# Source rows of a graph layer: the 45 tiles read row by row through SyncE go to GpSimd's gathers

## The chip, the core and the metric

The kernel runs on one core of a Trainium2 chip. The metric is the device time of one launch in microseconds. The chip's engines are named as the profile names them: PE (TensorE, matmuls; PEld is its weight load), DVE (VectorE), ACT (ScalarE), POOL (GpSimd) and SP (SyncE, which only issues DMAs here).

## The reference, cut to what matters

```
h   = relu(layernorm(x))                       # x: 12500 nodes x 48
tmp = concat([h[dst], h[src], edge_attr], 1)   # 400000 edges, dst sorted
msg = relu(tmp @ W1 + b1) @ W2 + b2            # W1: 128 x 128, W2: 128 x 48
out = x + segment_sum(msg, dst, 12500)
```

The edges are sorted by `dst`; `src` is random. So whatever depends on `dst` can be read in windows of neighbouring nodes, and whatever depends on `src` has to be picked node by node.

## The kernel before

**Two tables.** A first stage (`node_tables`, lines 92 to 232) normalizes the nodes and multiplies them by the two halves of W1. It leaves `tab_a` (destination half) and `tab_b` (source half), each one row of 128 numbers per node, in DRAM, and the source half a second time, turned, as `bt` in SBUF: 128 partitions, one column per node.

**Chunks.** The second stage (`windows`, lines 235 to 527) takes the edges in 3125 tiles of 128, eight tiles to a chunk, 391 chunks. For chunk c, SP loads a window of 80 rows of `tab_a` (`rhs`, line 362), the edge attributes (`lhs`, line 367) and the destinations (`row`, line 369). DVE makes one-hot windows of the destinations (`lhs`, line 383, and `hot`, line 388). PE multiplies `lhs` and `rhs` (line 401), which gives the destination and edge parts of eight tiles in PSUM (`pre`). The source part is added (lines 420 to 424), ACT applies relu (line 425), PE folds the edges into the 80 nodes of the window (`p_g`, lines 433 and 438), and DVE adds the window to a running segment (line 452). Segments of twelve chunks are multiplied by W2 and stored (lines 456 to 484).

**Three ways to the source rows of a tile.** The change is about these.

- *Gathers.* POOL issues one indirect DMA for a tile: 128 rows of `tab_b`, picked by the indices `srci`, go to one tile's place in `gb` (lines 375 to 381). 2719 tiles take this way. The pool of `gb` has six buffers of a chunk each, so POOL can start a chunk's gathers when `hid`, six chunks earlier, has read its buffer.
- *Columns.* In most chunks the last tile is put together from `bt`: each copy moves one column, at an address taken from a register, into `gt` (line 353). DVE does 59 of a chunk's 119 copies and ACT 60, and PE turns the tile onto `pre` (line 411). 361 tiles take this way (`BYCOLS`); their source part is in `pre` already, and ACT applies the relu straight from there (line 424).
- *Single rows.* SP reads one row of 512 bytes of `tab_b` into one partition of `gs`, with the address from a register (lines 314 to 325). It does 15 such DMAs in each chunk (`RPART`), so a tile of 128 rows is complete every eight or nine chunks. 45 tiles take this way (`BYROWS`, 5760 DMAs), and DVE adds such a tile by an instruction of its own (line 422).

**Numbers.** The registers are loaded from a table `last` in SBUF, one row of `WIDTH` int32 per chunk (line 304, at most 32 numbers a load). In a row stand the 119 column places, the base of the window and the 15 rows' nodes for SP (from `BASE` = 120 on), and four numbers for the segments. `SEG0` is the SBUF byte address of the first segment, which the tables' sizes shift.

**Order.** The order in each engine is written out by hand (lines 486 to 527): the loop body of chunk c issues `prepare(c)` (SP loads, gathers, one-hots, DVE's first 23 column copies), then the single rows of c, DVE's other column copies, the matmuls of c-1 and the fold of c-2, ACT's first 28 copies, `hidden(c-1)` (lines 415 to 426), ACT's other 32 copies and `add(c-2)`. The gathers that POOL issues meanwhile are for a chunk five or six further on.

Of the kernel before, what the change touches and what calls it, by code (L numbers as in the profile page):

```python
# [8 lines left out]
F32 = mybir.dt.float32  # L9
# [7 lines left out]
P = 128  # L17
N, D, DE, HID, E = 12500, 48, 32, 128, 400000
# [4 lines left out]
T = 8  # L23
# [20 lines left out]
U8 = mybir.dt.uint8  # L44
# [3 lines left out]


COLS = 1  # L50
ROWS0 = 1
END = NT // T


# [3 lines left out]
)  # L58
PART = sum(n for _, _, n, _ in PARTS)
BASE = 120  # L60
RPART = 15

BT0 = 16512
SEG0 = 122144
SEG_SIZE = 8 * L


SEG, NEXT, SEG2 = 136, 137, 138
PLACE0 = 139
WIDTH = 140  # L70
SLOTS = (NCH + 2 + P - 1) // P
MOST = 32

# [1 line left out]
def tiles_of(first, part):  # L75

    n = (END - first) * part // P
    return [first + (P * (j + 1) + part - 1) // part - 1 for j in range(n)]


BYCOLS = tiles_of(COLS, PART)
BYROWS = tiles_of(ROWS0, RPART)
EPS = 1e-5


# [149 lines left out]
def windows(nc, tc, gp, bt, ident, idx, x_t, tab_a, tab_b, dst, edge_t, w1, w2s, b2s, out_t):  # L235
# [3 lines left out]
    with ExitStack() as es:  # L239
# [5 lines left out]
        gtp = es.enter_context(tc.tile_pool(name="gtp", bufs=3))  # L245
# [13 lines left out]
        for _, _, n, at in PARTS:  # L259
# [1 line left out]
                last[:, :, at : at + n], last[:, :, at : at + n], 4, BT0,  # L261
                op0=ALU.mult, op1=ALU.add,
            )
        rows_at = slice(BASE, BASE + 1 + RPART)
        nc.vector.tensor_scalar(
            last[:, :, rows_at], last[:, :, rows_at], 4 * HID, None, op0=ALU.mult
        )
        tab8, taba8 = (t.rearrange("n h -> (n h)").bitcast(U8) for t in (tab_b, tab_a))

        place = PARTS[0][3] - 1  # L270
        for a, b in ((place, SEG2), (NEXT, SEG)):
# [5 lines left out]
        nc.vector.scalar_tensor_tensor(  # L277
            last[:, :, at_place], last[:, :, at_place], 4.0, last[:, :, PLACE0 : PLACE0 + 1],
            op0=ALU.mult, op1=ALU.add,
# [8 lines left out]
            rhss.append(rhs)  # L288
        st = {}
        gts = {}  # L290
        gss = {}

        def group(c):

            return divmod(c + OFF, GQ)
# [4 lines left out]
        def numbers(c, at, n, engine):  # L300

            got = []
            for k in range(0, n, MOST):
                got += nc.values_load_multi_w_load_instructions(  # L304
                    last[c % P : c % P + 1, c // P, at + k : at + min(k + MOST, n)],
                    engines=[engine], min_val=0, max_val=1 << 23,
                    skip_runtime_bounds_check_because="numbers of nodes, and what is made of them",
                )[1]
            return got

        def node(n):
            return n.with_bounds(min_val=0, max_val=N - 1)

        def rows(c, nodes):

            for k, n in enumerate(nodes):
                e = (c - ROWS0) * RPART + k
                of = BYROWS[e // P]
                if of not in gss:
                    gss[of] = gtp.tile([P, HID], F32, name="gs")  # L320
                n = n.with_bounds(min_val=0, max_val=4 * HID * (N - 1))
                nc.sync.dma_start(  # L322
                    gss[of].bitcast(U8)[e % P : e % P + 1, :],
                    tab8[bass.ds(n, 4 * HID)].rearrange("(o h) -> o h", o=1),
                )

        regs = {}

# [12 lines left out]
        def columns(c, part):  # L341

            dve, first, _, _ = PARTS[part]
            copy = nc.vector.tensor_copy if dve else nc.scalar.copy
            for k, at in enumerate(regs.pop((c, part), [])):
                j, e = divmod((c - COLS) * PART + first + k, P)
                of = BYCOLS[j]
                if of not in gts:
                    gts[of] = gtp.tile([HID, P], F32, name="gt")
                at = at.with_bounds(  # L350
                    min_val=BT0, max_val=BT0 + 4 * (N - 1), guaranteed_mod_val=0, out_of_modulus=4
                ) - BT0
                copy(gts[of][:, e : e + 1], bt8[:, bass.ds(at, 4)].bitcast(F32))  # L353

        def prepare(c):
            n = min(T, NT - c * T)
            at = c * CE
            m = max(0, min(RPART, len(BYROWS) * P - (c - ROWS0) * RPART)) if c >= ROWS0 else 0
            base, *nodes = numbers(c, BASE, 1 + m, mybir.EngineType.SP)
            rhs = rhss[c % 3]  # L360
            base = base.with_bounds(min_val=0, max_val=4 * HID * (N - 1))
            nc.sync.dma_start(
                rhs.bitcast(U8)[:W, :],
                taba8[bass.ds(base, 4 * HID * W)].rearrange("(w h) -> w h", w=W),
            )
            lhs = ld.tile([P, CE], F32, name="lhs")
            nc.sync.dma_start(lhs[W:K, : n * P], edge_t[:, at : at + n * P])
            row = ld.tile([W, CE], I16, name="row")
            nc.sync.dma_start(
                row[:, : n * P],  # L370
                dst[at : at + n * P].rearrange("(o e) -> o e", o=1).to_broadcast([W, n * P]),
            )
            st[c] = dict(n=n, rows=nodes)
            gb = gp.tile([P, T, HID], F32, name="gb")
            for t in range(n - (c in BYCOLS) - (c in BYROWS)):
                nc.gpsimd.indirect_dma_start(  # L376
                    out=gb[:, t, :], out_offset=None, in_=tab_b[:, :],
                    in_offset=bass.IndirectOffsetOnAxis(
                        ap=srci[:, c * T + t : c * T + t + 1], axis=0
                    ),  # L380
                )

            nc.vector.tensor_scalar(  # L383
                lhs[:W, : n * P], row[:, : n * P], bw[:, c : c + 1], None, op0=ALU.is_equal,
            )
            columns(c, 0)
            hot = wp.tile([P, T, W], F32, name="hot")
            nc.vector.tensor_tensor(  # L388
                hot[:, :n, :], wnum.unsqueeze(1).to_broadcast([P, n, W]),
                rel[:, c * T : c * T + n].unsqueeze(2).to_broadcast([P, n, W]), op=ALU.is_equal,  # L390
            )
            load(c, 1)
            st[c].update(rhs=rhs, lhs=lhs, gb=gb, hot=hot)
# [21 lines left out]
        def hidden(c):  # L415
            s = st[c]
            n, m, pre = s["n"], s["added"], s["pre"]
            h = wp.tile([P, T, HID], F32, name="hid")
            g = m - (c in BYROWS)
            nc.vector.tensor_add(h[:, :g, :], pre[:, :g, :], s["gb"][:, :g, :])  # L420
            if g < m:
                nc.vector.tensor_add(h[:, g, :], pre[:, g, :], gss.pop(c))
            if m < n:
                nc.scalar.activation(h[:, m, :], pre[:, m, :], AF.Relu)  # L424
            nc.scalar.activation(h[:, :m, :], h[:, :m, :], AF.Relu)  # L425
            s["h"] = h
# [16 lines left out]
        def add(c):  # L443

            s = st.pop(c)
            k = group(c)[0] % 2
            of = SEG0 + k * SEG_SIZE
            at = s["base"].with_bounds(
# [33 lines left out]
        def segment_store(g, n):  # L482
            first, = numbers(begin(g), SEG, 1, mybir.EngineType.SP)
            nc.sync.dma_start(out_t[:, bass.ds(node(first), n)], xs.pop(g)[:, :n])

        with tc.manual_schedule():
            for c in range(NCH + 2):
                if c < NCH:
                    prepare(c)
                    rows(c, st[c].pop("rows"))  # L490
                if c >= NCH:
                    columns(c, 0)
                columns(c, 1)
                load(c, 2)
                columns(c, 2)
                if 0 <= c - 1 < NCH:
                    before(c - 1)
                if 0 <= c - 2 < NCH:
                    fold(c - 2)
                if 0 <= c - 1 < NCH:  # L500
                    turned(c - 1)

                g, k = group(c - 2)
                if k == GQ - 3 or c == NCH - 1:
                    segment_load(g)
                if g > 0 and k < L // BLK:
                    segment_sum(g - 1, k, BLK)
                if g > 0 and k == STORE:
                    segment_store(g - 1, L)
                columns(c, 3)  # L510
                if 0 <= c - 1 < NCH:
                    hidden(c - 1)
                load(c + 1, 0)
                load(c, 4)
                columns(c, 4)
                if 0 <= c - 2 < NCH:
                    add(c - 2)
                    if k == GQ - 1:
                        segment_next(g)
                load(c + 1, 3)  # L520
                if c == NCH + 1:
                    segment_sum(g, 0, END_L)
                    segment_store(g, END_L)

                if c < PIECES:
                    s = slice(c * PIECE, (c + 1) * PIECE)
                    nc.sync.dma_start(out_t[:, s], x_t[:, s])
# [126 lines left out]
def tile_gnn_preln(  # L654
# [52 lines left out]
    flag = const.tile([1, 1], I32, name="flag")  # L707
    last = const.tile([P, SLOTS, WIDTH], I32, name="last")

# [157 lines left out]
```

## Time and profile before

| | |
|---|---|
| median of 3 runs | 5037.61 us (5035.85 to 5037.8) |
| the profiled execution | 5046.97 us, span 5045.2 us, granted PE clock 0.643 |
| first `hid` add (line 420) of 391 | at 158.51 us |
| last one | at 5032.55 us |
| busy | PE 63%, ACT 58%, DVE 58%, POOL 53% |
| gathers (line 376) | 2719, 972 ns each |
| SP's single rows (line 322) | 5760 of 0.5 KB |

All but 171 us of the span lies between these two adds: the loop over chunks. This text calls the time from the start of one `hid` add of DVE to the start of the next a **cycle**: one chunk. The 390 cycles have a mean of 12.50 us. No engine is busy for more than two thirds of the span, so the page's sums don't say what bounds the loop, and a cycle has to be read in the timeline. Column copies have a line of their own (353) on ACT and on DVE. "issue" in a wait is idle time in which the engine waited for nothing that the profile shows.

### The profile page before, as it was taken

Reading aid. Unit: us, or ns where it says so; the run is one execution under the profiler, and the core shown is the slowest. Engines: PE = TensorE matmul, PEld = TensorE weight load, DVE = VectorE, ACT = ScalarE, POOL = GpSimd, SP = SyncE. Lnnn points to the kernel's source line nnn. Section 1 sums busy time; section 2 is a strip of 40 time slices with the busy share of each in tenths; the row PEclk is TensorE's granted clock in tenths of the full one; section 3 lists DMA queues with packets and bytes.
Section 4 is the critical chain, followed back from the end, with each engine's and each line's share of the span. In section 5 each row is a group of like instructions: output and inputs, shape, how many; then the busy total and the mean of one; then the engine's idle time right before and its main releaser. Section 6 shows DMA issues by size and latency. Waiting matters only on the chain. (4 is left out here: it accounts for less than half of the span.)

```text
span 5045.2 us, 105760 instructions
## 1 busy us (share of the span) xinstructions
PE 3196.2 (63%) x16917; PEld 2891.6 (57%) x16917; DVE 2915.2 (58%) x24786; ACT 2927.7 (58%) x24107; POOL 2664.5 (53%) x2746
## 2 busy tenths in 40 slices
PE   6565666665666665566666665666666666666676
PEld 4555555555555555556565555556555565555565
DVE  4555555555555555565555555555555565555555
ACT  3455655655555555566565555556565566555555
POOL 5455555555555555555555555555555555555553
PEclk8666666666666666666666666666666666665656
DMA  3422222222222222222222222222222222222221
GB/s 135 123 67 69 68 66 68 68 67 68 64 65 66 68 70 67 64 68 71 67 69 69 68 67 67 69 67 69 67 67 68 69 71 68 68 66 69 66 69 51
DMA packets 202255, 354.44 MB, mean 70 GB/s; under 512 B 70322, under 2 KB 108228, under 8 KB 200276
## 3 DMA queue, kind: packets, MB, share of 16 engines
q0 software_dynamic: 87040, 178.39, 14.2%
q1 hardware_dynamic: 114256, 169.09, 11.3%
q14 instruction: 560, 4.59, 0.3%
q8 instruction: 139, 2.28, 0.2%
q10 hardware_dynamic: 260, 0.10, 0.0%
HBM read 327.84 MB, written 22.07 MB: 69 GB/s over the span
## 5 line engine op out<-in xcount | busy, mean ns | idle before, releaser
L376 POOL DMA_INDIRECT gb<-tab_b,srci x2719 | 2643.0, 972 | 2315.4 <-DVE hid L420 1319.5
L353 ACT COPY gt<-bt 128x1 f32 x23280 | 2477.9, 189 | 1893.8 <-issue 1867.1
L353 DVE COPY gt<-bt 128x1 f32 x22928 | 1704.1, 143 | 1795.4 <-issue 1750.0
L433 PE MATMUL p_g<-hot,hid 128*128 128x80 f32 x6250 | 1392.9, 414 | 1664.1 <-ACT hid L425 1585.3
L433 PEld LDWEIGHTS p_g<-hot,hid 128*128 128x128 f32 x6250 | 1313.3, 320 | 1745.7 <-ACT hid L425 1689.4
L401 PEld LDWEIGHTS pre<-rhs,lhs 112*128 112x128 f32 x6250 | 1149.6, 283 | 92.8 <-issue 85.4
L401 PE MATMUL pre<-rhs,lhs 112*128 112x128 f32 x6250 | 1171.3, 366 | 17.1 <-DVE lhs L383 17.1
L420 DVE TENSOR_TENSOR hid<-pre,gb 128x896 f32<-128x896 f32 (+2 forms) x391 | 420.8, 1076 | 6.8 <-issue 4.4
L425 ACT ACTIVATE hid<-hid 128x896 f32<-128x896 f32 (+1 forms) x391 | 370.8, 948 | 39.3 <-DVE hid L420 38.0
L411 PE MATMUL pre<-ident,gt 128*128 128x128 f32 x722 | 278.7, 489 | 112.0 <-remote 104.9
L388 DVE TENSOR_TENSOR hot<-wnum,rel 128x640 f32<-128x640 f32 x391 | 315.9, 808 | 5.1 <-issue 4.9
L383 DVE TENSOR_SCALAR lhs<-row,bw 80x1024 f32<-80x1024 int16 x391 | 306.8, 785 | 12.8 <-DMA row<-in_dst 7.9
L438 PEld LDWEIGHTS <-ones 128*128 128x128 bf16 x3125 | 291.9, 154 | 0.0
L438 PE MATMUL p_g<-hot,ones 128*128 128x80 bf16 x3125 | 283.7, 265 | 0.0
L411 PEld LDWEIGHTS pre<-ident,gt 128*128 128x128 f32 x722 | 193.4, 328 | 118.4 <-remote 110.6
L452 DVE TENSOR_TENSOR seg<-seg,p_g 128x160 f32 x391 | 125.7, 321 | 191.8 <-DVE hid L420 156.8
L424 ACT ACTIVATE hid<-pre 128x128 f32<-128x128 f32 x361 | 97.5, 270 | 86.8 <-DVE hid L420 78.4
L478 PE MATMUL p_f<-seg,w2s 128*48 128x512 f32 (+1 forms) x134 | 121.0, 1005 | 0.4 <-DVE seg L452 0.4
L479 PE MATMUL p_f<-seg,b2s 1*48 1x512 f32 (+1 forms) x134 | 95.5, 801 | 0.0
L479 PEld LDWEIGHTS p_f<-seg,b2s 1*48 1x48 f32 x134 | 13.1, 143 | 100.8 <-issue 100.8
L468 DVE MEMSET seg<- 128x944 f32 x64 | 54.1, 845 | 9.5 <-issue 0.3
L480 DVE TENSOR_TENSOR xseg<-xseg,p_f 48x512 f32<-48x512 f32 (+1 forms) x67 | 44.8, 668 | 23.3 <-PE p_f L479 22.4
(67 smaller groups left out, 306.3 us busy)
## 6 DMA issues: line engine op xcount, KB each, us to landing
gs<-tab_b SPq DMA_DIRECT2D x5760, 0.5 KB
row<-in_dst SPq DMA_DIRECT2D x390, 160.0 KB
lhs<-in_edge_t SPq DMA_DIRECT2D x390, 128.0 KB
gb<-tab_b,srci POOLq DMA_INDIRECT x2719
rhs<-tab_a SPq DMA_DIRECT2D x391, 40.0 KB
xseg<-in_x_t SPq DMA_DIRECT2D x33, 192.0 KB
out_x<-xseg SPq DMA_DIRECT2D x33, 192.0 KB
tab_b<-tab SPq DMA_DIRECT2D x3, 1280.0 KB
```

The source lines that it names most:

```text
L353: copy(gts[of][:, e : e + 1], bt8[:, bass.ds(at, 4)].bitcast(F32))
L376: nc.gpsimd.indirect_dma_start(out=gb[:, t, :], out_offset=None, in_=tab_b[:, :], in_offset=bass.IndirectOffsetOnAxis(ap=srci[:, c * T + t ...
L383: nc.vector.tensor_scalar(lhs[:W, : n * P], row[:, : n * P], bw[:, c : c + 1], None, op0=ALU.is_equal,)
L388: nc.vector.tensor_tensor(hot[:, :n, :], wnum.unsqueeze(1).to_broadcast([P, n, W]), rel[:, c * T : c * T + n].unsqueeze(2).to_broadcast([P ...
L401: nc.tensor.matmul(pre[:, t, :], s["lhs"][:K, t * P : (t + 1) * P], s["rhs"][:K, :], start=True, stop=c not in BYCOLS or t < n - 1,)
L411: nc.tensor.matmul(s["pre"][:, s["n"] - 1, :], gts.pop(c), ident, start=False, stop=True)
L420: nc.vector.tensor_add(h[:, :g, :], pre[:, :g, :], s["gb"][:, :g, :])
L425: nc.scalar.activation(h[:, :m, :], h[:, :m, :], AF.Relu)
L433: nc.tensor.matmul(p_g[:, 0, :], s["h"][:, t, :], s["hot"][:, t, :], start=t == 0, stop=t == n - 1)
L438: nc.tensor.matmul(p_g[:, 1, :], ones, high[:, t, 1::2], start=t == 0, stop=t == n - 1)
L452: nc.vector.tensor_add(to, to, s["p_g"])
L478: nc.tensor.matmul(p_f[:, :n], w2s, seg[:, 0, s], start=True, stop=False)
```

## The change

The single rows go: `rows()`, its list of tiles `BYROWS`, the 15 extra numbers per chunk that SP loads, and the separate add. The 45 tiles are gathered by POOL as the others are, so there are 2764 gathers. The add of line 422 becomes part of that of line 420. The row of numbers in `last` shrinks from 140 int32 to 128 (of which the base takes one and three are left empty), its segment numbers move, and `SEG0` becomes 192 bytes less (four rows of twelve int32 less on each partition).

```diff
-RPART = 15
-SEG0 = 122144
+SEG0 = 121952
-SEG, NEXT, SEG2 = 136, 137, 138
-PLACE0 = 139
-WIDTH = 140
+SEG, NEXT, SEG2 = 124, 125, 126
+PLACE0 = 127
+WIDTH = 128
...
-        def rows(c, nodes):
-
-            for k, n in enumerate(nodes):
-                e = (c - ROWS0) * RPART + k
-                of = BYROWS[e // P]
-                if of not in gss:
-                    gss[of] = gtp.tile([P, HID], F32, name="gs")
-                n = n.with_bounds(min_val=0, max_val=4 * HID * (N - 1))
-                nc.sync.dma_start(
-                    gss[of].bitcast(U8)[e % P : e % P + 1, :],
-                    tab8[bass.ds(n, 4 * HID)].rearrange("(o h) -> o h", o=1),
-                )
...
-            m = max(0, min(RPART, len(BYROWS) * P - (c - ROWS0) * RPART)) if c >= ROWS0 else 0
-            base, *nodes = numbers(c, BASE, 1 + m, mybir.EngineType.SP)
+            base, = numbers(c, BASE, 1, mybir.EngineType.SP)
...
-            for t in range(n - (c in BYCOLS) - (c in BYROWS)):
+            for t in range(n - (c in BYCOLS)):
                 nc.gpsimd.indirect_dma_start(
...
-            g = m - (c in BYROWS)
-            nc.vector.tensor_add(h[:, :g, :], pre[:, :g, :], s["gb"][:, :g, :])
-            if g < m:
-                nc.vector.tensor_add(h[:, g, :], pre[:, g, :], gss.pop(c))
+            nc.vector.tensor_add(h[:, :m, :], pre[:, :m, :], s["gb"][:, :m, :])
...
-                    rows(c, st[c].pop("rows"))
```

What SP issues early in the loop shows the first place; `rhs`, `lhs` and `row` are the loads of a chunk, `gs` the single rows, and line 304 is the load of the registers. Before, for chunk 1:

```order
L304 TENSOR_LOAD last
L362 DMA rhs_703<-tab_a 80x512
L367 DMA lhs<-in_edge_t 32x1024
L369 DMA row<-in_dst 80x1024
L322 DMA gs<-tab_b 1x512 x15
L527 DMA out_x<-in_x_t 48x1696
```

Of the change, at the same place:

```order
L300 TENSOR_LOAD last
L344 DMA rhs_703<-tab_a 80x512
L349 DMA lhs<-in_edge_t 32x1024
L351 DMA row<-in_dst 80x1024
L505 DMA out_x<-in_x_t 48x1696
```

Nothing else moved in SP's list: 5760 issues have gone from between the loads of one chunk and of the next, and the register load ahead of them reads one number in place of 16.

DVE's part of the loop at the first tile of single rows (chunk 9), before:

```order
L388 TENSOR_TENSOR hot<-wnum,rel 128x640
L304 TENSOR_LOAD last
L353 COPY gt<-bt 128x1 x20
L304 TENSOR_LOAD last
L353 COPY gt<-bt 128x1 x16
L420 TENSOR_TENSOR hid<-pre,gb 128x768
L422 TENSOR_TENSOR hid<-pre,gs 128x128
L304 TENSOR_LOAD last
L452 TENSOR_TENSOR seg_660<-seg_660,p_g 128x2x80
```

Of the change:

```order
L370 TENSOR_TENSOR hot<-wnum,rel 128x640
L300 TENSOR_LOAD last
L336 COPY gt<-bt 128x1 x20
L300 TENSOR_LOAD last
L336 COPY gt<-bt 128x1 x16
L401 TENSOR_TENSOR hid<-pre,gb 128x896
L300 TENSOR_LOAD last
L431 TENSOR_TENSOR seg_660<-seg_660,p_g 128x2x80
```

One add of seven tiles stands where an add of six and one of a single tile stood; the column copies and the register loads of DVE and ACT are the same. In POOL's list the count of gathers in a row goes from 2719 to 2764.

More of the change, by code (lines that the diff above doesn't have):

```diff
@@ L50 @@
 COLS = 1
-ROWS0 = 1
 END = NT // T
@@ L81 @@
 BYCOLS = tiles_of(COLS, PART)
-BYROWS = tiles_of(ROWS0, RPART)
 EPS = 1e-5
@@ L263, in windows @@
             )
-        rows_at = slice(BASE, BASE + 1 + RPART)
+        rows_at = slice(BASE, BASE + 1)
         nc.vector.tensor_scalar(
@@ L267, in windows @@
         )
-        tab8, taba8 = (t.rearrange("n h -> (n h)").bitcast(U8) for t in (tab_b, tab_a))
+        taba8 = tab_a.rearrange("n h -> (n h)").bitcast(U8)
         place = PARTS[0][3] - 1
@@ L290, in windows @@
         gts = {}
-        gss = {}
         def group(c):
@@ L372, in prepare @@
             )
-            st[c] = dict(n=n, rows=nodes)
+            st[c] = dict(n=n)
             gb = gp.tile([P, T, HID], F32, name="gb")
-            for t in range(n - (c in BYCOLS) - (c in BYROWS)):
+            for t in range(n - (c in BYCOLS)):
                 nc.gpsimd.indirect_dma_start(
@@ L827 @@
         numbers[COLS : COLS + len(cols), at : at + n] = cols[:, k : k + n]
-    in_rows = np.array(BYROWS) * T + T - 1 - np.isin(BYROWS, BYCOLS)
-    rows = by_tile[in_rows].reshape(-1)
-    rows = np.pad(rows, (0, -len(rows) % RPART)).reshape(-1, RPART)
-    numbers[ROWS0 : ROWS0 + len(rows), BASE + 1 : BASE + 1 + RPART] = rows
     last = np.ascontiguousarray(numbers.reshape(SLOTS, P, WIDTH).transpose(1, 0, 2))
```

## The prediction

> **What bounds the kernel now.** I read the costliest groups of the page first, then the waits, then single cycles in the timeline.
>
> ```profile
> L376 POOL DMA_INDIRECT gb<-tab_b,srci x2719 | 2643.0, 972 | 2315.4 <-DVE hid L420 1319.5
> L353 ACT COPY gt<-bt 128x1 f32 x23280 | 2477.9, 189 | 1893.8 <-issue 1867.1
> L353 DVE COPY gt<-bt 128x1 f32 x22928 | 1704.1, 143 | 1795.4 <-issue 1750.0
> gs<-tab_b SPq DMA_DIRECT2D x5760, 0.5 KB
> ```
>
> The reader is to see two things. POOL is not saturated: it sits idle for 1319.5 us until a `hid` add gives a buffer back. And the column copies have as much idle time before them as work in them, although they wait for nothing that the profile shows. Where this idle time lies is seen in one cycle. Here is DVE from 1736.74 us, and what SP issues in it:
>
> ```profile
> 1736.74 1.07 DVE L420 TENSOR_TENSOR hid<-pre,gb 128x896 f32<-128x896 f32 x1
> 1740.22 0.81 DVE L388 TENSOR_TENSOR hot<-wnum,rel 128x640 f32<-128x640 f32 x1
> 1741.16 0.58 DVE L353 COPY gt<-bt 128x1 f32 x8
> 1742.37 0.22 DVE L353 COPY gt<-bt 128x1 f32 x2 [0.63 <-issue]
> ...
> 1744.53 0.15 DVE L353 COPY gt<-bt 128x1 f32 x1 [0.52 <-issue]
> ...
> 1747.39 0.15 DVE L353 COPY gt<-bt 128x1 f32 x1 [0.52 <-issue]
> 1748.13 1.18 DVE L353 COPY gt<-bt 128x1 f32 x18 [0.58 <-issue]
> 1749.82 1.08 DVE L420 TENSOR_TENSOR hid<-pre,gb 128x896 f32<-128x896 f32 x1
> ```
> ```profile
> 1738.17 10.48 SPq L322 DMA_DIRECT2D gs<-tab_b  x15
> ```
>
> Eight copies run at full pace (0.58 us for eight). Then, until 1748.13, one or two pass every 0.71 us or so: I call this the **crawl**. It ends at once, and the 18 copies that are left run at full pace up to the `hid` add. ACT's copies show the same steps. SP's 15 single rows take 10.48 us in this cycle, 0.7 us each; six of them outside a crawl took 1.83 us (a row below), 0.3 us each. So SP crawls too.
>
> The crawl goes with the gathers. POOL's gathers follow each other every 1.25 us, and a burst starts when `hid` is done:
>
> ```profile
> 1280.64 0.95 POOL L376 DMA_INDIRECT gb<-tab_b,srci  x1 [5.75 <-DVE hid L420]
> 1281.89 0.94 POOL L376 DMA_INDIRECT gb<-tab_b,srci  x1 [0.30 <-issue]
> ...
> 1288.15 0.95 POOL L376 DMA_INDIRECT gb<-tab_b,srci  x1 [0.30 <-issue]
> 1292.89 0.95 POOL L376 DMA_INDIRECT gb<-tab_b,srci  x1 [3.79 <-DVE hid L420]
> ```
>
> In the next cycle that I show, the crawl ends at 1290.63, 1.53 us after the last of these gathers (1288.15 + 0.95). And in whole cycles (first and last of each kind; the number after x under POOL counts its gathers):
>
> ```profile
> core 0: us, PE busy (x) PEld busy (x) DVE busy (x) ACT busy (x) POOL busy (x), PEclk, DMA share, GB/s
> 170.97:183.87 12.90, 7.74 (x42) 7.55 (x42) 7.37 (x65) 7.54 (x66) 6.89 (x7) 0.62 0.38 103
> 4969.55:4981.66 12.11, 5.52 (x35) 5.08 (x34) 6.84 (x65) 7.52 (x65) 6.89 (x7) 0.64 0.30 83
> 196.25:207.25 11.00, 7.25 (x42) 7.06 (x42) 6.94 (x65) 6.96 (x61) 5.95 (x6) 0.69 0.37 97
> 4908.49:4918.99 10.50, 9.41 (x49) 8.92 (x48) 6.93 (x64) 6.23 (x50) 6.20 (x6) 0.52 0.33 89
> 5000.29:5007.87 7.58, 5.87 (x54) 5.48 (x53) 6.47 (x65) 6.50 (x61) 0.00 (x0) 0.99 0.14 40
> ```
>
> Of all cycles, 323 have seven gathers and a mean of 12.63 us, 39 have six and 11.38 us. Without gathers, at the end of the loop, the same DVE and ACT work takes 7.58 us. So the loop is a ring: `hid` frees a buffer, the burst runs, DVE and ACT crawl through most of it, then finish their copies, and the next `hid` follows. What bounds a cycle is the burst, plus what copies are left when the crawl ends.
>
> **The change part by part.**
>
> *45 more gathers.* Each makes the cycle in which it is issued 1.25 us longer: that is the spacing of two gathers (1281.89 − 1280.64), and also 12.63 − 11.38. 45 × 1.25 = **+56 us**. Nothing hides it, since the burst is on the ring. By the lowest price it is nothing (POOL idles for longer than that), by the highest 1.5 us (12.11 − 10.50 is 1.6): 0 to +72. I take 56, the price of both rows.
>
> The Trainium skill, "Perfetto Trace Analysis", section "Identifying the Most-Contended Engine", judges POOL by its occupancy and would have me optimize the engine with the highest one. By it POOL, the least busy here with 53%, takes the gathers for nothing and the sum below would be 56 us lower; the cycles of six and of seven gathers speak against it.
>
> *45 adds less.* One add of 128x896 takes 1.08 us. The pair that stood in its place is this, at 4981.66 us:
>
> ```profile
> 4981.66 0.95 DVE L420 TENSOR_TENSOR hid<-pre,gb 128x768 f32<-128x768 f32 x1
> 4982.52 0.28 DVE L422 TENSOR_TENSOR hid<-pre,gs 128x128 f32<-128x128 f32 x1
> ```
>
> It ends 1.14 us after its start, so 0.06 us is saved 45 times: **−3 us**. This is on the ring.
>
> *5760 issues less on SP.* Nobody waits for SP by name, as these waits show:
>
> ```profile
> POOL gb L376 <- DVE hid L422: 165.9, 44, 5.7
> DVE lhs L383 <- DMA row<-in_dst: 7.9, 1, 7.9
> DVE lhs L383 <- DMA gs<-tab_b: 4.3, 2, 3.9
> ```
>
> (The first is the ring itself in the chunks of single rows; it will stand under L420's successor.) Taken from waits, SP's work is worth 12 us at most. But SP crawls along with DVE and ACT, and I found cycles in which SP issued nothing. Here SP waits from 1278.1 to 1291.64 us for a segment to store, at the same place of the twelve chunks as the cycle shown above:
>
> ```profile
> 1276.29 1.83 SPq L322 DMA_DIRECT2D gs<-tab_b  x6
> 1291.64 0.35 SPq L484 DMA_DIRECT2D out_x<-xseg  x1
> ```
> ```profile
> 1279.30 1.08 DVE L420 TENSOR_TENSOR hid<-pre,gb 128x896 f32<-128x896 f32 x1
> 1282.69 0.81 DVE L388 TENSOR_TENSOR hot<-wnum,rel 128x640 f32<-128x640 f32 x1
> 1283.61 1.46 DVE L353 COPY gt<-bt 128x1 f32 x20
> ...
> 1290.63 0.40 DVE L353 COPY gt<-bt 128x1 f32 x5 [0.56 <-issue]
> 1291.54 1.07 DVE L420 TENSOR_TENSOR hid<-pre,gb 128x896 f32<-128x896 f32 x1
> ```
>
> With SP quiet, 20 copies pass before the crawl in place of 8, and 5 are left behind it in place of 18. The cycle takes 12.24 us against 13.08. There are five such quiet cycles with seven gathers (first 1279.30, last 4747.59 us): mean 12.32. The other 23 at this place have a median of 12.98: **−0.66 us** for a wholly quiet SP.
>
> After the change SP is not wholly quiet; it still loads a chunk's `rhs`, `lhs` and `row`. What that looks like stands at the end of the trace, when the single rows have run out:
>
> ```profile
> 4951.62 6.34 SPq L322 DMA_DIRECT2D gs<-tab_b  x10
> ...
> 4969.84 0.33 SPq L362 DMA_DIRECT2D rhs<-tab_a  x1
> ...
> 4971.81 0.33 SPq L461 DMA_DIRECT2D xseg<-in_x_t  x1
> ```
>
> The cycle from 4969.55 us (above) has seven gathers and an SP that issues its loads at the start and nothing in the crawl: 12.11 us, where the 267 cycles of seven gathers at the ten ordinary places of twelve have a mean of 12.39: **−0.28 us**. The cycle before it (4957.07 to 4969.55 us), in which SP issued the loads of two chunks, took 12.48 us and shows no gain. So the gain of a cycle lies between 0 and 0.66. I take the nearest rows: 0.28 for the ten ordinary places, whose cycles will look like this one, and 0.66 for the two places (of twelve) where the segment's matmuls lengthen the cycle, which is where the quiet cycles stand. Gathers are issued in 385 cycles: 321 × 0.28 + 64 × 0.66 = 90 + 42 = **−132 us**. At the ends, 0 and 385 × 0.66 = −254.
>
> *The table and the address of the segments.* The register loads of DVE and ACT keep their counts. Shorter rows could change what one load takes:
>
> ```profile
> L304 ACTq TENSOR_LOAD <-last x776: 1695/1932/2829, 134.8 to 5009.0; - x194
> ```
>
> Chunks lie in four rows of 560 bytes on a partition, at four different distances from a round address; the medians of ACT's loads in the first three are 1929, 1923 and 1912 ns. So I count nothing for the 512-byte rows. SP's load of 16 numbers becomes a load of one; SP has the time. The 3 MB that SP read come by POOL's gathers instead, with the same bytes, and the DMA engines are under 40% busy in every cycle shown above.
>
> *Sum.* +56 − 3 − 132 = **−79 us**. The profiled execution took 5046.97 us, 9.4 over the median of the runs. Against the median: 5037.61 − 79 = **4959 us**.
>
> **The rivals.**
>
> *SP's issues cost the others nothing* (the time gets longer). Then the quiet cycles are short for another reason: at that place SP waits just when DVE is late with the segment, so they may have been picked by DVE's own state. For it: the cycle from 4957 us, with SP out of the crawl and no gain. Against it: the 12 more copies before the crawl, in a cycle whose one-hot (`hot`) stands 3.4 us after `hid` as in the other (3.5 us). Price: +56 − 3 = +53, 5091 us. It decides as soon as a quiet SP is worth less than 53/385 = 0.14 us a cycle. The Trainium skill, "DMA: Bandwidth & Descriptors", section "Issuing engines are not separate DMA queues", holds that issuing from several engines only saves time on the sequencer that issues. By that rule SP's time, which nobody waits for, is worth nothing, and 5091 us follows; the quiet cycles of this trace disagree by 0.66 us each.
>
> *The quiet cycle is the rule everywhere.* SP's loads fall outside the crawl, and every cycle gains 0.66: −254 + 53 = −201, 4837 us. For it: some 45 ordinary cycles are over 13.2 us, and in the ones I looked at SP's single rows start early in the burst; these would go. Against it: the cycle from 4969.55.
>
> *All copies fit under the burst.* Then a cycle is 1.34 us to the first gather (1280.64 − 1279.30), 8.46 us to the end of the seventh, 1.53 us to the crawl's end: 11.3 us, and 385 cycles give over 400 us. Against it: ACT has 60 copies of some 0.09 us and two relus of 1.2 us, and does not get through them faster than 12.1 us in the cycle from 4969.55.
>
> *The change does nothing but what hides*, and gain and price cancel: within 0.2%.
>
> **How the numbers follow.** My forecast (4959 us, its own range 4900 to 5020) has 0.55, SP without worth 0.24, the quiet cycle everywhere 0.12, all copies under the burst 0.04, a cancellation 0.05. The range takes in the first three: 4830 to 5095 us. A measurement of this kernel can tell about 0.2% from no change, 10 us. Faster by over that: 0.55 + 0.12 + 0.04, less some of the forecast's upper edge, 0.70; within it 0.06; slower 0.24.
>
> **What would show it.** In the new profile, gathers still 1.25 us apart, 2764 of them, and nearly all cycles with seven. If a quiet SP is worth something, more copies pass on DVE between `hot` and the crawl (over 12), fewer than 10 are left when it ends, and an ordinary cycle is near 12.1 us. If SP is worth nothing, ordinary cycles stay at 12.4 us and the time goes up by the gathers alone. The prediction is wrong in its ground if the crawl no longer ends 1.5 us after the last gather, or if the burst no longer starts with `hid`: then POOL or another engine bounds the loop. If DVE waits for `row`, SP's loads come late.

## The result and the profile after

The changed kernel takes 4972.71 us (median of four runs, 4970.34 to 4976.2) against 5037.7 us before: a ratio of 0.9857, with a 95% interval of 0.9833 to 0.9881, or 65 us less. The profiled execution took 4973.7 us with a span of 4972.0 us. That is 73.2 us less than the span of before, of which 9.3 us are what the profiled execution of before lay above its median.

One fact has to be known before any further number is read. All twelve runs that follow were made on five chips, and on all five the kernel *before* takes 3568 to 3579 us and not 5037 us. There the crawl doesn't appear, and there the change makes the kernel slower. What sets the two conditions apart isn't known, nor whether the chip of before and after is one of the five; I call them the **crawling** condition (the runs of before and of the change above) and the **flowing** one. The granted PE clock is lower in the crawling traces (0.643 and 0.644, against 0.762 and 0.752 in the flowing traces of the same two kernels). By itself that is no mark of the crawl: a slower kernel on a flowing chip, the one with rows of 125 numbers below, gets 0.58 in its slow part, where PE is 48% busy, and 0.76 ahead of it, where PE is 75% busy.

First the crawling condition. The page of the changed kernel, its groups of gathers and copies:

```profile
L358 POOL DMA_INDIRECT gb<-tab_b,srci x2764 | 2682.8, 971 | 2202.5 <-DVE hid L401 1438.1
L336 ACT COPY gt<-bt 128x1 f32 x23280 | 2476.5, 187 | 1843.6 <-issue 1817.5
L336 DVE COPY gt<-bt 128x1 f32 x22928 | 1708.5, 143 | 1715.5 <-issue 1634.7
```

There are 45 gathers more, each as long as before, and POOL still waits for `hid`. Before, that wait was 1319.5 us for the add of line 420 and 165.9 us for that of line 422, 1485.4 us together; now it is 1438.1 us, 47 us less. The copies wait for nothing visible for 115 us less on DVE (1634.7 for 1750.0) and 50 us less on ACT. The timeline shows how. This is DVE in the cycle of the chunk whose cycle the prediction shows for before (the one from 1736.74 us there):

```profile
1703.71 1.08 DVE L401 TENSOR_TENSOR hid<-pre,gb 128x896 f32<-128x896 f32 x1
1705.79 1.47 DVE L336 COPY gt<-bt 128x1 f32 x23
1707.18 0.81 DVE L370 TENSOR_TENSOR hot<-wnum,rel 128x640 f32<-128x640 f32 x1
1708.13 1.34 DVE L336 COPY gt<-bt 128x1 f32 x20
1709.97 0.15 DVE L336 COPY gt<-bt 128x1 f32 x1 [0.51 <-issue]
1710.71 0.21 DVE L336 COPY gt<-bt 128x1 f32 x2 [0.58 <-issue]
...
1714.30 0.15 DVE L336 COPY gt<-bt 128x1 f32 x1 [0.50 <-issue]
1715.00 0.46 DVE L336 COPY gt<-bt 128x1 f32 x6 [0.55 <-issue]
1715.97 1.08 DVE L401 TENSOR_TENSOR hid<-pre,gb 128x896 f32<-128x896 f32 x1
```

POOL's gathers in it, the first and the last of seven:

```profile
1705.05 0.95 POOL L358 DMA_INDIRECT gb<-tab_b,srci  x1 [5.59 <-DVE hid L401]
...
1712.56 0.94 POOL L358 DMA_INDIRECT gb<-tab_b,srci  x1 [0.30 <-issue]
```

After `hot`, 20 copies now pass before the crawl where 8 did, and 6 are left behind it where 18 were. This cycle is one of those with a segment's matmuls; the part on the prediction says how far the others are like it. SP issues nothing between 1703.71 and 1715.97 us, where it issued its 15 rows. The crawl still ends 1.50 us after the last gather (1712.56 + 0.94 to 1715.00). The cycle takes 12.26 us for 13.08.

### The profile page after: what moved, and what is told of

It reads as the page before. It is cut to its first block, busy times and chain, and to the rows that moved or that the text cites. A ratio compares the mean times of both kernels' runs of the same rounds, so it can differ in the third digit from the quotient of the medians.

```text
span 4972.0 us, 94216 instructions
## 1 busy us (share of the span) xinstructions
PE 3217.5 (65%) x16917; PEld 2903.8 (58%) x16917; DVE 2921.8 (59%) x24741; ACT 2925.2 (59%) x24107; POOL 2704.3 (54%) x2791
## 3 DMA queue, kind: packets, MB, share of 16 engines
q1 hardware_dynamic: 102736, 166.09, 11.2%
## 4 chain that ended last, share of the span: by engine, by line
issue 37%; DVE 24%; POOL 21%; ACT 8%; PE 3%; DVEq 3%; DMA 2%; another core or an unknown queue 1%; ACTq 1%; SPq 0%; POOLq 0%
POOL gb L358 21%; DVE gt L336 14%; ACT gt L336 7%; DVE hid L401 3%; DVE lhs L365 3%; DVEq L300 3%; DVE hot L370 2%; DMA gb<-tab_b,srci 1%; ACT hid L404 1%; PE p_g L412 1%; PE p_n L178 1%; PE pre L383 1%; ACTq L300 1%; DVE seg L431 1%
## 5 line engine op out<-in xcount | busy, mean ns | idle before, releaser
L358 POOL DMA_INDIRECT gb<-tab_b,srci x2764 | 2682.8, 971 | 2202.5 <-DVE hid L401 1438.1
L336 DVE COPY gt<-bt 128x1 f32 x22928 | 1708.5, 143 | 1715.5 <-issue 1634.7
L401 DVE TENSOR_TENSOR hid<-pre,gb 128x896 f32<-128x896 f32 (+1 forms) x391 | 426.7, 1091 | 7.8 <-issue 6.7
L393 PE MATMUL pre<-ident,gt 128*128 128x128 f32 x722 | 278.0, 488 | 64.3 <-remote 57.5
```

The lines of the kernel that those rows point to most:

```text
L358: nc.gpsimd.indirect_dma_start(out=gb[:, t, :], out_offset=None, in_=tab_b[:, :], in_offset=bass.IndirectOffsetOnAxis(ap=srci[:, c * T + t ...
L393: nc.tensor.matmul(s["pre"][:, s["n"] - 1, :], gts.pop(c), ident, start=False, stop=True)
L401: nc.vector.tensor_add(h[:, :m, :], pre[:, :m, :], s["gb"][:, :m, :])
```

## The experiments

### Single rows and gathers, each by itself

Four kernels were made from the kernel before. The first drops the rows and keeps the six gathers of the 45 chunks:

```
-                    rows(c, st[c].pop("rows"))
-                nc.vector.tensor_add(h[:, g, :], pre[:, g, :], gss.pop(c))
+                nc.vector.tensor_add(h[:, g, :], pre[:, g, :], zrow)
```

> The kernel before without SP's 5760 single rows; the 45 chunks still gather six tiles and still add in two pieces, the second from a tile of zeros (the source part of these 45 tiles is left out). Theory (SP's issues lengthen the crawl): the change moved the time by -65 us; with +53 us for gathers and adds, the quiet SP is worth -118 us, so 4920 us here, in a span of 4905 to 4935; ordinary cycles of seven gathers near 12.08 us, those of six below the 11.38 us of before. Rival (SP's issues cost the others nothing): 5037 us, and the gain of the change came from gathers taking the place of rows.

The second keeps the rows, into tiles that nobody reads, and gathers and adds as the changed kernel does; the third and the fourth change its rows:

```
-            for t in range(n - (c in BYCOLS) - (c in BYROWS)):
+            for t in range(n - (c in BYCOLS)):
...
-            for k, n in enumerate(nodes):
+            for k, n in enumerate(nodes[:8]):
...
-                    tab8[bass.ds(n, 4 * HID)].rearrange("(o h) -> o h", o=1),
+                    tab8[bass.ds(n, 4 * HID * RPART)].rearrange("(o h) -> o h", o=RPART),
```

> The changed kernel's gathers and adds, with the 15 single rows a chunk still issued by SP into tiles that nobody reads. Theory: the gathers alone, 5037.6 + 53 = 5090 us, or 4973 + 118; ordinary cycles of seven gathers back at 12.39 us. Rival (the issues cost nothing): 4973 us, as changed. Rival (gathers cost nothing, POOL has idle time): 5037 us.

> As the run with all 15 rows added, but with the first eight of a chunk only. Theory, if every issue has the same price: 4973 + 118 x 8/15 = 5036 us. Rival (only issues that reach the crawl cost, and the first six or so pass ahead of it at 0.3 us each): two or three of fifteen count, about 4990 us.

> As the run with all 15 rows added, but the 15 rows are one transfer of 15 neighbouring rows with one issue (the same 7.5 KB in the same 15 lines of 512 bytes). Theory (the instruction on SP is what costs): 4973 + 118/15 = 4981 us. Rival (the transfers cost, by their bytes and packets): 5090 us.

Measured, with the kernel before at 3578.58 us beside them:

| kernel | gathers | SP's rows in a chunk | us | ratio to before (95%) |
|---|---|---|---|---|
| no rows | 2719 | none | 3579.85 | 1.0008 (0.9998 to 1.0017) |
| rows added | 2764 | 15 | 3630.87 | 1.0162 (1.0136 to 1.0189) |
| half of the rows | 2764 | 8 | 3635.95 | 1.0165 (1.0148 to 1.0182) |
| rows as one transfer | 2764 | 1 issue, 15 lines | 3634.43 | 1.0168 (1.0149 to 1.0187) |

In the flowing condition the gathers alone set the time: 52 us more with them (3630.87 − 3578.58), and the three kernels with the same gathers and different rows lie within each other's intervals. The theory's numbers (4920 and 5090 us) can't be compared with these, since the condition is another; of its two terms the gathers' is there and SP's is zero. The rival's ratios (1 for no rows) came true.

### The changed kernel in the flowing condition

> The changed kernel as it is. The four runs so far ran where the kernel before takes 3579 us and shows no crawl: ACT's and DVE's copies keep their pace through the bursts, and SP's rows are issued 0.32 us apart. If the run is made in that condition: theory (the gathers are the bound and cost 1.25 us each, a quiet SP is worth nothing there): 3579 + 53 = 3632 us, slower. If the run is made where the kernel before takes 5037 us: 4973 us, as measured. Rival (the change gains by something that is not the crawl): about 65 us faster in both.

> The kernel before as it is, for a trace in whatever condition this chip has. Where it takes 3570 to 3580 us: no crawl, POOL's gathers nearly back to back, 2719 of them, cycles near 8.83 us against 8.97 of the changed kernel (57 us in 385 cycles). Where it takes 5037 us: the trace of before again.

Measured: 3630.37 us for the change against 3569.88 us, a ratio of 1.0177 (1.0150 to 1.0203): **the change is slower there**, by 60 us. The kernel before took 3568.26 us in its own run. These are two traces to set beside those of the crawling condition. First the groups of the kernel before, flowing:

```profile
L376 POOL DMA_INDIRECT gb<-tab_b,srci x2719 | 2651.9, 975 | 862.7 <-issue 803.4
L353 ACT COPY gt<-bt 128x1 f32 x23280 | 2235.0, 187 | 574.7 <-issue 442.0
L353 DVE COPY gt<-bt 128x1 f32 x22928 | 1497.0, 142 | 263.8 <-issue 223.2
```

A gather and a copy take as long as in the crawling trace (972, 189 and 143 ns there). The unexplained idle time of the copies is 442.0 and 223.2 us in place of 1867.1 and 1750.0, and the largest wait of POOL, for `hid`, is gone: what is left is 0.30 us between two gathers. The chain that ended last says the same, before and changed:

```profile
POOL 50%; issue 25%; DVE 9%; DMA 5%; PE 5%; ACT 4%; DVEq 1%; SPq 1%; ACTq 0%; POOLq 0%
```
```profile
POOL 59%; issue 27%; DMA 6%; DVE 5%; PE 2%; DVEq 1%; ACT 0%; ACTq 0%; POOLq 0%; SPq 0%
```

The ring has opened: POOL gathers without a pause and is the bound. Here are DVE and SP in one flowing cycle of before, that of the next chunk after the one shown above:

```profile
1201.97 1.08 DVE L420 TENSOR_TENSOR hid<-pre,gb 128x896 f32<-128x896 f32 x1
...
1206.58 0.81 DVE L388 TENSOR_TENSOR hot<-wnum,rel 128x640 f32<-128x640 f32 x1
1207.46 1.30 DVE L353 COPY gt<-bt 128x1 f32 x20
1209.26 1.06 DVE L353 COPY gt<-bt 128x1 f32 x16 [0.49 <-issue]
1210.24 1.08 DVE L420 TENSOR_TENSOR hid<-pre,gb 128x896 f32<-128x896 f32 x1
```
```profile
1205.87 4.83 SPq L322 DMA_DIRECT2D gs<-tab_b  x15
```

Gathers run all through this cycle, and SP issues 15 rows in it, 0.32 us each; still 20 and 16 copies pass at full pace. So gathers and rows together don't suffice for a crawl. The cycles have a mean of 8.82 us before and 8.97 us in the change, as expected (8.83 and 8.97).

The first and the last gather of the loop stand at 50.69 and 3544.14 us before, at 50.60 and 3607.19 us in the change. That is 1.285 us for each of 2718 intervals, and 1.287 us for each of 2763. The 45 gathers cost 45 x 1.29 = 58 us, and the rest of the 63 us is the slightly longer interval.

### SP's instructions without transfers

The changed kernel, with this in each chunk:

```
+            for k in range(30):
+                nc.sync.reg_mov(spare, k)
```

> The changed kernel with 30 register moves a chunk on SP, which nobody reads, and no transfers. Where the kernel before takes 5037 us: 5090 us if SP's instructions are what lengthens the crawl, 4973 us if it is the transfers. Where it takes 3570 us: 3630 us in either case, since SP waits for a buffer most of a chunk.

Measured: a single run of 3625.6 us beside 3575.51 us of before (ratio 1.014). It tells nothing of the crawl. The kernel with all rows added was run once more as well:

> The gathers and adds of the changed kernel with SP's 15 single rows a chunk still issued, once more, in case this chip is one on which the kernel before takes 5037 us. If it is: theory (SP's issues lengthen the crawl) 5090 us; rival (they cost nothing) 4973 us. If the kernel before takes 3570 to 3580 us: 1.016 of it, as in the first such run.

It gave 3624.8 us against 3570.76 us, 1.0151 (1.0104 to 1.0198), in the flowing condition again.

### Six gathers in a chunk

```
-            for t in range(n - (c in BYCOLS)):
+            for t in range(min(6, n)):
...
+            for t in range(6, m):
+                nc.vector.tensor_add(h[:, t, :], pre[:, t, :], zrow)
```

> The changed kernel with six gathers at most in every chunk; the seventh tile adds zeros on DVE (its source part is left out), and the eighth too in the chunks that gathered eight. 415 gathers fewer and about 390 adds of 0.28 us more. Theory (the stream of gathers is the bound where the kernel before takes 3575 us): 415 x 1.25 = 519 us off 3630, less what DVE adds, but not below the 7.6 us a cycle that the same DVE and ACT work takes without gathers: 3110 to 3220 us. Rival (DVE or ACT is the bound): 3630 + 390 x 0.28 = 3740 us. Where the kernel before takes 5037 us: 4973 - 519 + 109 = 4560 us by the ring, 4973 or more if POOL had time to spare.

Measured: 3355.36 us, 0.9397 of before (0.9356 to 0.9437). 419 gathers fewer took off 275 us, 0.66 us each: neither the theory's 410 to 520 us nor the rival's loss. The chain that ended last and one wait of this kernel show why:

```profile
ACT 53%; issue 14%; DVE 13%; PE 9%; ACTq 3%; DVEq 2%; POOL 1%; DMA 1%
```
```profile
POOL gb L358 <- DVE hid L403: 341.7, 319, 20.2
```

POOL waits for `hid` again, and ACT is the bound at 8.27 us a cycle, not at the 7.6 us that I had taken from a cycle without gathers. So in the flowing condition ACT stands at most 0.7 us a cycle behind POOL (8.97 us); the added add on DVE, which ACT's relu waits for, is part of the 8.27 us.

### More columns in place of gathers

The kernel before, with 127 columns in a chunk in place of 119 (and the table 8 numbers wider):

```
-    (True, 0, 23, 1), (True, 23, 20, 24), (True, 43, 16, 44),
-    (False, 59, 28, 60), (False, 87, 32, 88),
+    (True, 0, 27, 1), (True, 27, 20, 28), (True, 47, 16, 48),
+    (False, 63, 32, 64), (False, 95, 32, 96),
```

> The kernel before, with 127 columns copied in a chunk in place of 119 (four more on DVE, four more on ACT), so that 24 more tiles come from the node table on the chip and 24 fewer from gathers; SP's single rows stay. Where the kernel before takes 3570 us, theory (the stream of gathers is the bound, DVE and ACT have idle time): 24 x 1.25 = 30 us less, 0.9916 of before. Rival (DVE or ACT bounds it): 8 more copies, 4 x 0.07 us on DVE in 390 cycles, 25 us more. Where it takes 5037 us (the crawl): the gathers give 30 us back, and four more copies on each engine that wait for the crawl's end cost 0.3 us in 390 cycles, over 100 us more.

Measured: 3533.37 us against 3577.41 us, 0.9877 (0.9860 to 0.9893). In the flowing condition this is faster than both kernels of the case, by 44 us where 30 were expected (the rival's 25 us is a slip: 4 x 0.07 us in 390 cycles is 109 us), and its chain shows that ACT's reserve is now used up:

```profile
ACT 47%; issue 16%; DVE 13%; PE 10%; POOL 8%; ACTq 2%; DVEq 2%; DMA 2%; SPq 1%; POOLq 0%
```

It wasn't run in the crawling condition.

### The table: rows of 125 numbers, and the table alone

The changed kernel without the padding:

```
-SEG0 = 121952
+SEG0 = 121904
...
-SEG, NEXT, SEG2 = 124, 125, 126
-PLACE0 = 127
-WIDTH = 128
+SEG, NEXT, SEG2 = 121, 122, 123
+PLACE0 = 124
+WIDTH = 125
```

> The changed kernel with rows of 125 numbers in place of 128 (no padding; the same numbers in the same order, the segments' address 48 bytes lower). My prediction counts nothing for the table: 1.0177 times the kernel before where that takes 3570 us, 0.9857 times where it takes 5037 us. Rival (the alignment is worth something): ACT's and DVE's register loads get longer than the 1.9 and 1.1 to 1.6 us of before in three of four rows, and 0.2 us or more a chunk, 80 us or more in all, is added.

Measured: 5895.13 us, 1.6474 of before (1.6446 to 1.6501), 2265 us above the padded change. The rival was right in kind, and its 80 us were far too low a floor. The register loads by engine (lowest, median and highest in ns), in rows of 128 numbers and of 125:

```profile
L300 DVEq TENSOR_LOAD <-last x1202: 307/1382/5175, 104.4 to 3615.1; - x172
L300 ACTq TENSOR_LOAD <-last x776: 1721/1954/3490, 91.3 to 3586.8; - x194
L300 SPq TENSOR_LOAD <-last x459: 266/275/478, 94.3 to 3615.9; - x153
```
```profile
L300 DVEq TENSOR_LOAD <-last x1202: 306/3717/6305, 104.6 to 5879.4; - x172
L300 ACTq TENSOR_LOAD <-last x776: 1714/6189/7421, 91.4 to 5848.9; - x194
L300 SPq TENSOR_LOAD <-last x459: 263/274/482, 94.5 to 5880.1; - x153
```

The loads of many numbers get three times as long, SP's load of one doesn't change. And DVE's and ACT's busy share over the span shows when:

```profile
DVE  6888777743333333333333333333333333333333
ACT  5887777743333333333333333333333333333333
```

Within a row, every run of numbers starts a multiple of 16 bytes from the row's start. The first 128 chunks, whose numbers lie in the first row of each partition (at 0 bytes), run as in the padded kernel; from chunk 128 on (500, 1000 and 1500 bytes, that is 4, 8 and 12 over a multiple of 16) every load is slow, with means of 6.57, 6.57 and 6.46 us on ACT.

The aligned table by itself, in the changed kernel with the 45 chunks' gathers and adds as before (zeros for the row's part):

```
-            for t in range(n - (c in BYCOLS)):
+            for t in range(n - (c in BYCOLS) - (c in BYROWS)):
...
+            if g < m:
+                nc.vector.tensor_add(h[:, g, :], pre[:, g, :], zrow)
```

> The changed kernel's table (rows of 128 numbers, SP loading one number a chunk) and no single rows, but with six gathers and the add in two pieces in the 45 chunks, as before the change (zeros are added for the source part of these 45 tiles). Where the kernel before takes 3570 to 3580 us: equal to it (ratio 0.999 to 1.002) if the table costs nothing and only the gathers do; 1.015 if the 60 us come from the table and not from the gathers. Where it takes 5037 us: 5037 - 118 = 4919 us if a quiet SP is worth what the change's result leaves for it, 5037 us if it is worth nothing.

Measured: 3579.93 us against 3578.16 us, 1.0007 (0.9998 to 1.0017). From 140 numbers to 128, and from SP's load of 16 to a load of one, the time doesn't move.

## Why the prediction was right, and where it was not

*The time* was forecast as 4959 us and came out at 4972.7 us, inside the forecast's own range. That holds for the crawling condition alone, which the prediction took for the nature of the kernel.

*The ground: ring, burst and crawl.* In the trace of the change the signs of the ground are there: 2764 gathers, 1.25 us apart in a burst, started by `hid` and followed 1.5 us later by the crawl's end. Over all cycles with seven gathers, 10.9 copies are left on DVE when the crawl ends, 14.6 before; I had said fewer than 10. The other sign, over 12 copies between `hot` and the crawl, tells the two kernels apart less well than I thought: at the ten ordinary places the median is 14 in the change and 14 before as well. But "the crawl goes with the gathers" was taken as cause, and the flowing traces show the same gathers at the same spacing without it. The trace of before held a hint that I passed over. Ahead of the loop, gathers run while `tab_a` is still being made, and SP has no single rows to issue yet; its first stand here:

```profile
147.72 5.38 SPq L322 DMA_DIRECT2D gs<-tab_b  x15
```

These are the stretches from 50 to 66 us and from 66 to 100 us, crawling and then flowing, in the columns PE, PEld, DVE, ACT and POOL busy, granted clock, DMA share and GB/s:

```profile
50.00:66.00 16.00, 15.52 (x41) 6.87 (x40) 9.52 (x10) 9.31 (x11) 11.44 (x13) 1.00 0.18 46
66.00:100.00 34.00, 9.51 (x23) 5.24 (x22) 2.68 (x3) 2.32 (x3) 25.77 (x28) 0.58 0.20 53
```
```profile
50.00:66.00 16.00, 15.53 (x40) 6.88 (x39) 9.45 (x10) 9.31 (x11) 11.65 (x13) 1.00 0.17 46
66.00:100.00 34.00, 22.98 (x103) 19.05 (x101) 13.98 (x25) 12.41 (x44) 25.77 (x28) 0.87 0.78 285
```

In the first stretch, with 13 gathers, the two traces do the same work: even in the crawling condition the first gathers run without a crawl. In the second, with 28, POOL still does the same, while PE, DVE and ACT get 23, 3 and 3 instructions done in place of 103, 25 and 44. PE stands there for 20.1 us ahead of its matmuls (line 181), waiting for nothing that the profile shows. One copy with a fixed address waits almost 21 us for nothing visible in the crawling trace:

```profile
98.89 0.69 DVE L188 COPY tab<-p_n 128x512 f32<-128x512 f32 x1 [20.93 <-issue]
```

If this is the same stall as in the loop, the crawl needs neither SP's rows nor copies addressed by registers, and it isn't bound to DVE and ACT. The gathers' transfers take as long in both conditions, and so do those of the queue named "instruction", so longer transfers aren't what sets the conditions apart. The queues of before, crawling and flowing, with packets, MB and their share of 16 engines' span:

```profile
q0 software_dynamic: 87040, 178.39, 14.2%
...
q14 instruction: 560, 4.59, 0.3%
```
```profile
q0 software_dynamic: 87040, 178.39, 19.8%
...
q14 instruction: 560, 4.59, 0.4%
```

14.2% of 5045.2 us is 716 us, 19.8% of 3566.5 us is 706 us; for q14 it is 15 and 14 us. What the crawl is stays open.

*45 more gathers, +56, and 45 adds less, −3.* (The highest price of a gather is 1.6 us, as in 12.11 − 10.50 and in the +72, and not 1.5.) Right where they could be measured apart, in the flowing condition: +52 and +54 us with the rows kept, +60 us in the change itself, against the +53 us of the sum. A quiet SP alone, and a quiet SP with the new table, gave 1.3 and 1.8 us there, inside their intervals. In the crawling condition the two terms weren't measured alone.

*A quiet SP, −132.* Right in size by subtraction: 65 + 53 = 118 us by the medians, 73 + 53 = 126 us by the spans. By place, cycles of seven gathers went from 12.39 to 12.08 us at the ten ordinary places (0.31 where 0.28 was predicted), from 14.44 to 14.13 us at one segment place (0.31 for 0.66) and from 13.14 to 12.41 us at the other (0.73 for 0.66): the one that I had read the price from. 321 x 0.31 + 32 x 0.31 + 32 x 0.73 = 133 us. There is luck in this. The 0.28 rests on one cycle of 12.11 us, and a third of before's ordinary cycles, nearly all with SP issuing its rows, are as short as that; the 0.73 has two cycles of 16.63 and 18.11 us in before's mean, though the medians, 12.89 and 12.24 us, give 0.65.

How it was earned is, at most places, not what I read from the quiet cycle. (The crawl is taken here as the runs of at most three copies, parted by over 0.4 us from one copy's start to the next.) At the place of the quiet cycles the median of the copies between `hot` and the crawl does go from 13 to 20. At the ordinary places it stays at 14, and the crawl doesn't start later: 4.5 us after the first gather, in the median of both kernels. But more gets through in it. Between 4.5 us after the first gather's start and 1.3 us after the last one's end, an ordinary cycle of before passes 8.7 copies on DVE, 8.0 on ACT and 3.9 issues of SP on the mean; one of the change passes 10.8, 10.5 and none. The sum is nearly the same, 20.6 and 21.3, as if DVE and ACT had taken SP's places. Against this reading, cycles of before in which SP issued more there don't have fewer copies (three issues: 7.5 on DVE and 7.3 on ACT, 77 cycles; five issues: 11.2 and 9.6, 35 cycles).

So that a quiet SP earned it is argued, not shown: it fits these counts, and no other part of the change can be worth that much if the table is worth as little as in the flowing runs. The experiments that would have told it apart (rows without gathers, gathers without rows) all fell into the other condition, where a quiet SP is worth nothing.

*The table, 0.* Right between 140 and 128 numbers. But I wrote it off by comparing rows that were all aligned, and never priced the padding itself: without it the change would have taken 1.65 times as long.

*The rival that SP's issues cost nothing* had 0.24 and a price of +53 us. In the crawling condition it came out false: 65 us less where it says 53 more. It is what happens on all five chips of the experiments, with its number (+60 us). The rule of the Trainium skill that I had set against my rows, "DMA: Bandwidth & Descriptors", section "Issuing engines are not separate DMA queues" (issuing from several engines only saves time on the sequencer that issues), agrees with every flowing run: 15 issues, 8, one or none a chunk, with the same gathers, lie within 1.0151 and 1.0177 of before. Judging by occupancy (the Trainium skill, "Perfetto Trace Analysis", section "Identifying the Most-Contended Engine") fails there too: POOL, 75% busy, is the bound in the flowing trace of before, beside ACT and DVE at 76%.

The step that failed is therefore one: "The crawl goes with the gathers" was read from one trace as a law of the kernel, and it held only in the condition of that trace.

## What to carry to other kernels

When engines that "wait for nothing the profile shows" stand still for longer than they work, get a second trace of the same kernel, on another chip if there is one, before building on it: this one took 5037 us in one condition and 3568 to 3579 us on five chips, and a change that gains 1.4% in the one costs 1.8% in the other. Work taken from an engine that is off the critical path helps only while it shares something with the path; put a price on both cases and say which sign hangs on it. Where an engine loads a run of numbers from SBUF into registers, keep the start of each run on a multiple of 16 bytes.

## What the runs showed of the hardware that I had not expected

**Register loads and alignment.** In an aligned row ACT's loads of 28 and 32 numbers take about 1.75 and 2.0 us; in rows that start 4, 8 or 12 bytes off, about 6.1 and 7.0 us, or 0.22 us a number. DVE's loads of 16, 20 and 24 numbers go from 1.1, 1.4 and 1.6 us to 3.7, 4.6 and 5.4 us, 0.23 us a number. Aligned, four more numbers cost 0.25 us. That looks like one read for 16 bytes when aligned and one for each number when not, which is an inference. The Trainium skill, "Runtime: NRT & Kernel Launch", section "Instruction fetch mechanics", gives about 200 ns a register, even for many, for the register loads that the runtime adds. The loads here read SBUF; the unaligned ones come near to that with 0.22 us, the aligned ones take 0.06 us.

**Gathers beside a DVE comparison.** In the flowing trace of before, 240 of 2719 gathers take longer than 1.05 us, and all of them overlap with the comparison that makes `lhs`. One pair, where 0.94 us is usual:

```profile
1204.63 1.44 POOL L376 DMA_INDIRECT gb<-tab_b,srci  x1 [0.30 <-issue]
```
```profile
1204.52 0.74 DVE L383 TENSOR_SCALAR lhs<-row,bw 80x1024 f32<-80x1024 int16 x1
```

Another 279 gathers overlap with it and aren't longer than 1.05 us; what counts is when it runs. Where it starts 0.2 us before the gather, the gather takes 1.37 us (median of 44), where both start together, 0.94 us (median of 25). The 240 cost POOL 78 us over the usual time, 0.32 us each, and since POOL is the bound there, that is on the path. In the kernel with more columns it is 180 gathers and 57 us; these 20 us (77.8 − 57.5) and 24 x 1.25 = 30 us more than account for the 44 us that it gained. The Trainium skill, "SBUF — State Buffer", section "SBUF: two separate sides", says that GpSimd can't write a gather's descriptors while certain operations of DVE hold a port that they share; these rows agree in direction, though no run here shows which of DVE's operations hold the port.
